# Attention scores as one-pass float32r products of exact 12-bit halves, in a transformer-like block on one Trainium2 core

## The chip, the cores and the metric

The kernel runs on one core of a Trainium2 chip. The metric is the device time of one execution in microseconds, the median over runs. TensorE (PE) multiplies matrices into eight PSUM banks, VectorE (DVE), ScalarE (ACT) and GpSimd (POOL) work on tiles, and SyncE (SP) issues the DMAs. Each engine takes its own instructions in order and waits on semaphores for the others.

## What is computed

For 16 batches of 256 positions with 256 channels, all in float32: masked attention with 16 heads of 16 channels, a normalisation with a condition's shift and gain, a time mix with two running sums over the positions, a residual, a rotation of the channels, and a gated feed-forward layer whose inputs and weights are rounded to a four-bit grid in blocks of 16. Cut to what the change touches:

```python
q, k, v = (proj(Wq), proj(Wk), proj(Wv))                  # [B, 16 heads, 256, 16]
scores = jnp.einsum('bhsd,bhtd->bhst', q, k) * scale      # scale = 16 ** -0.5
scores = jnp.where(mask[None, None, :, :], -jnp.inf, scores)
attn = jax.nn.softmax(scores, axis=-1)
out = jnp.einsum('bhst,bhtd->bhsd', attn, v)
...
out = out @ Wo.T                                           # then norm, shift and gain
...
x = x + _L0_attn_ref(_L0_cond_ref(x, ...), ...)            # time mix
x = x + _L0_ffn_ref(_L0_cond2_ref(x, ...), ...)            # rotation, feed-forward
```

The four-bit rounding makes the result sensitive to small errors ahead of it, so the products are made in full float32 throughout the kernel before.

## The kernel before

Each batch passes through nine stages, written as Python generators that yield after every few instructions. The stages are: `ask` (load x, turn it so that channels lie on partitions, project q, k and v), `attend` (scores, exponentials, products with v, division), `leave` (output projection and normalisation), `mix` (three projections, two scans, a reciprocal of 128x512), `rotate` (a projection, a rotation, rounding to the grid), `hidden` for each half of the positions (gate, up, tanh, products, rounding), `turn_h` for each half (transposes), and `down` (the last projection and the output's DMA).

What runs when is written out by hand in the text `ORDER`: 1735 steps such as `t4` (the next piece of `attend` for batch 4) or `i2` (`hidden`, second half's generator of batch 2: `h` and `i` are the two halves, `d` and `e` their transposes, `a` ask, `l` leave, `m` mix, `r` rotate, `f` down; capitals are the setup). The loop over `ORDER.split()` calls `next` on the stage named. Every engine's queue, SP's too, has its instructions in this order; several batches are on their way at the same time. Between them lie pools of buffers. PSUM has two pools of four banks: `ps_s` for scores alone, `ps_g` for all else.

In `ask`, the projection of q (L567, through `project`) goes to ScalarE twice (L626): once with the odd heads of each pair set to zero and once with the even ones (`parq`), with the factor `QSCALE`. k is copied once (L632). `attend` has a function `scores(g, kt, w)`, called four times a batch. It takes all four banks of `ps_s`. One of its four products (L656) is 32 rows, which are two heads, by 128 keys by 512 columns, which are the 256 queries of the one head and the 256 of the other. The four products stand on different rows of the array. ScalarE then takes the exponential of each bank into `w` (L665). `values` (L677) multiplies with v and a column of ones; the division follows on DVE. `qT` and `kT` have two buffers each, and `w` has two, each for both key halves of a group of eight heads.

After the last batch the kernel reads `within`, which `check` has computed from all sums of exponentials (in range or not, and whether the mask is the same for all queries). If it is 0, the whole computation runs again in the function `exact`. With the inputs given it is 1.

`load_x` (L143) and the stores of `down` (L949, L931) are issued by SP, four DMAs of 64 KB a batch each, or, for the last three batches, two of 128 KB.

Of the kernel before, what the change touches and what calls it, by code (L numbers as in the profile page):

```python
# [8 lines left out]
F32 = mybir.dt.float32  # L9
BF16 = mybir.dt.bfloat16  # L10
I32 = mybir.dt.int32
# [6 lines left out]
P = 128  # L18
# [9 lines left out]
L L L L L W1 L L a0 W5 Q Q a0 Q Q K a0 W1 W1 K K Q W1 Q L W1 a0 R a0 K a0 L W5 R L W0 W1 K K K W5 A R t0 a0 L A  # L28
W1 O t0 L a0 W3 R W5 W5 W0 M a1 A O t0 A W5 a1 R M a2 W5 t0 t0 t0 a1 R a1 t0 W0 W3 t0 R W3 W3 t0 W2 a1 t0 t0 a1
M a1 t1 a1 W0 A W3 V0 t1 t1 R R A M t0 W0 W3 a2 R t1 W0 V0 M t1 W2 t1 t0 W3 t1 t1 W4 a3 V1 W0 t0 A t0 M t0 t1 V0  # L30
t0 a3 t0 A T W2 W2 t1 T t1 V0 t1 a2 a2 a2 t1 l0 a2 t1 a2 t1 V0 l0 l0 t1 V0 a2 W4 W2 t1 l0 V0 a4 l0 l0 t2 l0 m0
t1 V1 W4 a3 t2 t2 a3 a3 m0 m0 m0 m0 m0 t2 t2 a3 W4 V1 t2 m0 m0 m0 l1 l1 l1 m0 m0 m0 l1 t2 W4 m0 m0 m0 m0 m0 t2
t2 t2 t2 l1 V0 l1 l1 a3 a3 V0 t2 t2 r0 V1 t2 W4 m1 m1 t2 W2 m1 m1 r0 a4 m1 t3 m1 W4 t3 t2 m1 m1 V1 t2 t3 t3 t2
W2 V1 r0 t3 t3 m1 m1 m1 m1 r0 V1 a4 l2 l2 m1 m1 m1 m1 t3 m1 a4 r0 t3 l2 t3 t3 a4 t3 t3 l2 r1 r1 r0 t3 r0 a4 l2
t3 t3 r1 r1 r1 l2 l2 a4 a4 a5 t3 r0 r0 a5 r0 m2 m2 t4 t4 t3 t3 m2 m2 a6 i0 i0 i0 i0 t4 i0 i0 i0 i0 i0 i0 i0 i0
i0 i0 m2 m2 m2 m2 m2 r1 r1 r1 r1 m2 t4 t4 m2 t4 r1 m2 a5 a5 a5 a5 a5 a5 m2 l3 t5 l3 t4 l3 l3 h0 m2 m2 m2 t4 t5
m2 h0 h0 h0 h0 h0 h0 l3 h0 h0 h0 r2 t5 l3 l3 V1 h0 i1 h0 r2 t4 r2 a6 V1 h0 m3 t4 i1 a7 h0 r2 i1 h1 i1 r2 t4 h1
h1 i1 t4 h1 t4 t4 h1 h1 h1 t4 m3 m3 a6 h1 h1 t5 a6 h1 r2 h1 r2 t4 t5 t4 i1 a6 r2 r2 t5 h1 h1 i1 r2 m3 a6 t5 i1
i1 i1 i1 t5 t5 h1 m3 t5 t4 t5 t5 a6 a6 m3 m3 t6 t6 m3 m3 m3 i1 i1 m3 m3 i2 i2 i2 i2 i2 m3 e0 e0 i2 i2 t6 t6 e0
i2 l4 i2 t6 i1 i2 i2 t6 h2 h2 e0 t5 m3 m3 m3 l4 h2 t6 l4 h2 m3 h2 t6 l4 h2 i2 h2 h2 h2 h2 t5 r3 h2 t5 l4 r3 a7  # L40
d0 l4 t5 h2 t6 t5 t5 l4 i2 m4 d0 d0 m4 a8 h2 t6 d0 h2 i2 a7 r3 t6 a7 a7 t6 t6 t6 t6 a7 m4 m4 m4 r3 r3 a7 a7 m4
m4 m4 t7 l5 t7 t7 l5 m4 m4 m4 m4 m4 t6 t7 l5 l5 l5 r3 m4 m4 e1 m4 m4 l5 l5 t7 t6 t6 f0 f0 f0 f0 r4 t7 r3 r4 a8
r3 e1 e1 e1 r3 f0 t7 t7 t7 d1 d1 r4 t7 t7 d1 r3 r4 i3 a9 d1 r4 i3 m5 m5 i3 i3 i3 i3 i3 a8 r4 m5 m5 i3 i3 i3 t7
a8 a8 a8 i3 i3 i3 m5 m5 t8 m5 m5 m5 l6 l6 a8 a8 l6 r4 h3 h3 l6 t8 t8 m5 h3 h3 h3 f1 m5 m5 t8 t8 i3 l6 t8 h3 f1
m5 m5 h3 h3 t7 r4 r4 r4 f1 l6 m5 m5 l6 h3 h3 h3 m5 t8 t8 t7 t7 t7 t7 t8 r5 t8 f1 t8 i4 i4 m6 t8 t8 r5 a9 d2 h3
h3 i4 d2 i4 aa i4 t8 m6 h3 t8 m6 a9 r5 r5 r5 a9 a9 a9 t8 t9 t7 d2 r5 r5 t8 t9 m6 i4 d2 r5 r5 r5 i4 i4 i4 i4 e2
m6 e2 m6 a9 i4 e2 i4 t8 e2 a9 m6 m6 l7 i4 l7 m6 m6 m6 t9 l7 l7 f2 f2 m6 m6 m6 m6 l7 l7 l7 l8 l8 t9 h4 m7 h4 l8
h4 m6 l8 m6 m7 f2 h4 f2 h4 h4 h4 h4 r6 h4 h4 l8 m7 m7 t9 t9 r6 l8 l8 h4 t9 t9 t9 r6 aa e3 f1 r6 i4 i5 h4 t9 e3
e3 e3 h4 i5 i5 i5 i5 t9 m8 r6 i5 m7 i5 i5 h4 r6 aa m7 i5 aa t9 t9 t9 ab t9 m8 i5 i5 i5 d3 f2 m7 r6 d3 h5 h5 h5
h5 h5 aa aa h5 i5 r6 r6 ta t9 h5 t9 h5 m7 h5 ta ta h5 h5 m7 h5 aa ta r6 h5 m8 aa m7 d3 d3 m7 m7 m7 m7 h5 m7 f3  # L50
m7 m7 f3 f3 f3 m8 m8 ta ta ta m8 ta m8 ta r7 r7 m8 m8 m8 ta ta d4 d4 ta i5 ta ta ta ab f3 i6 i6 i6 i6 i6 i6 i6
i6 i6 i6 i6 h6 h6 h6 h6 h6 h6 h6 h6 h6 h6 i6 ab ab ab ab d4 d4 ta tb h6 m8 h6 t9 m8 e4 e4 i6 h6 ab m8 ta ta e4
m8 ac r7 m8 l9 tb m8 i6 ab e4 f4 f4 l9 r7 h6 r7 f4 l9 l9 l9 m8 e5 tb r8 tb f4 l9 l9 f4 r8 d5 ac m9 m9 m9 r8 e5
r8 r7 r7 tb m9 la d5 r7 la la m9 m9 r8 la ac ac m9 m9 m9 m9 m9 r8 r7 tb m9 d5 m9 r7 ac m9 la d5 la la m9 ac tb
m9 tb tb i7 ma ma tb tb ad i7 i7 i7 i7 i7 i7 i7 i7 e5 e5 i7 i7 i7 tb tc tc tc m9 r8 i7 f5 f5 i7 ma f5 f5 d6 f5
r8 d6 r9 tb h7 r9 tb h7 ad r8 tb ma r8 h7 h7 h7 h7 r9 r9 h7 h7 h7 ma ma tb r9 ma r9 tc tc tc tb h7 h7 h7 ad ad
tb r9 ac ac ma ma ma ma ma h8 h8 h8 tc ma ma d6 h8 h8 d6 tc ad i8 ma ma ad r9 i8 i8 i8 i8 i8 i8 h8 h7 h8 tc i8
i8 i8 h7 ma h8 e6 h8 e6 e6 e6 h8 lb h8 h8 r9 f6 lb i8 i8 r9 f6 h8 f6 f6 ra i8 lb lb lb f6 tc tc ra e7 lb lb e7
tc h8 i8 i9 tc i9 i9 i9 ae tc ra tc mb e7 i9 mb ad ra ra td d7 e7 i9 ad tc ra i9 ae d7 td td mb mb ra tc i9 tc
i9 mb td td h9 ra i9 mb i9 mb td mb h9 mb h9 i9 h9 h9 h9 mb h9 h9 h9 d7 d7 td h9 h9 td td i9 h9 h9 lc lc td lc  # L60
af mb ae ra mb lc f7 mb mb i9 ae lc lc ra mb f7 mb lc mc ia mc h9 ia ia ia ia f7 f7 ia ia ia td ia ia ia ia mb
rb rb td td d8 td ae rb f7 ia td rb ae ae mc d8 te td mc d8 mc ae rb ia d8 rb td e8 mc td mc mc af mc e8 e8 e8
mc mc mc rb mc ld mc mc f8 te mc te te rb rb ld ld ld te ha f8 f8 ha mc ha ha rb te ha f8 ha ha ha te ha ib ha
ha ha te te te te te ib ha rc ib ib ib ib ib ib ld ld ld te rc ha ib rc ib ib e9 hb d9 rc md e9 af te rc md hb
ib hb f8 te hb md hb ib e9 md d9 af te te af e9 hb rc rc ib rc te C md af hb hb hb hb hb d9 d9 tf md af af md rc
rc hb hb le le md md tf f9 tf le md md f9 le md tf md md md md md tf tf ic ic ic ic ic f9 f9 ic ic ic le hb rd
ic le ic tf ic rd le ic me f9 rd tf ic da tf rd rd da ea hc ea hc hc rd ea ic me hc da ea tf hc rd hc tf da me
me me me tf tf hc rd me hc hc tf tf hc hc me me hc me tf tf rd tf hc me fa me me me me fa fa rd db fa me lf id
db lf fa id id id id lf lf id id id me db id id id hc lf C hd hd lf db hd lf id hd hd eb re id eb eb hd hd mf mf
id eb hd re re hd fb re hd dc hd re fb fb mf re dc fb hd mf fb mf mf re hd mf ec ec ec dc dc mf ec re fc hd mf  # L70
fc mf fc mf mf ed re fc dd fc ed mf re dd mf mf mf mf ed ie ed ie ie ie ie ie ie ie dd rf dd ie ie he C he ie he
rf rf ie C rf he ie he ie he rf fd he he he rf rf rf fd he fd he rf ee fd rf if if he he if ee if if he if if if
if hf hf if hf if if hf ee ee fd hf if hf de if hf hf hf de de de hf hf fe hf hf fe hf fe fe ef ef ef fe ef ff df
df df df ff ff ff ff ff ff
# [4 lines left out]
def kernel(  # L79
# [38 lines left out]
    QSCALE = float(D) ** -0.5  # L118

# [136 lines left out]
    odd = const.tile([P, 1], F32, tag="odd", name="odd")  # L256

# [193 lines left out]
    good = const.tile([P, (B - 1) * 2 * H], F32, tag="good", name="good")  # L451
# [3 lines left out]
    def check():  # L455
        def meet(b0, b1, dst):
            r = recs[:, b0:b1].rearrange("p b g n -> p (b g n)")
            gd = good[:, 0 : (b1 - b0) * 2 * H]
            nc.vector.tensor_scalar(gd, r, LEAST, None, ALU.is_ge)
            nc.vector.scalar_tensor_tensor(gd, r, MOST, gd, ALU.is_lt, ALU.mult)  # L460
            nc.vector.tensor_reduce(dst, gd, AX.X, ALU.min)

        meet(0, B - 1, met[:, 0:1])
        yield
        meet(B - 1, B, met[:, 1:2])
        nc.vector.scalar_tensor_tensor(met[:, 1:2], odd, 0.5, met[:, 1:2], ALU.is_le, ALU.mult)
        nc.vector.tensor_tensor(met[:, 0:1], met[:, 0:1], met[:, 1:2], ALU.min)
        yield
        pb = ps()
        nc.tensor.transpose(pb[0:1, 0:P], met[:, 0:1], ident)  # L470
        yield
        top = const.tile([1, 1], F32, tag="top", name="top")
        nc.vector.tensor_reduce(top, pb[0:1, 0:P], AX.X, ALU.min)
        nc.vector.tensor_scalar(within, top, 0.5, None, ALU.is_ge)
        yield
# [140 lines left out]

    def ask(b):
        xT = yield from enter(b)
        srcs = [xT[:, 0, :], xT[:, 1, :]]
        pq = ps()  # L620
        project(pq, wT["q"], srcs)
        yield

        qT = att_p.tile([P, E2, 2, S], F32, tag="qT", name="qT", bufs=2)
        for i in range(2):
            nc.scalar.activation(qT[:, :, i, :], halves(pq), AF.Identity, scale=parq[:, i : i + 1])  # L626
        yield
# [3 lines left out]
        kT = att_p.tile([P, E2, S], F32, tag="kT", name="kT", bufs=2)  # L631
        nc.scalar.copy(flat(kT), pk)  # L632
# [13 lines left out]
    def attend(b):  # L646
        (qT, kT), vo = qks.pop(b), v_one[b % 2]

        def scores(g, kt, w):
            quad = [bank(ps_s, "pss") for _ in range(4)]
            for r in range(4):
                rows_ = slice(32 * r, 32 * r + 32)
                nc.tensor.matmul(  # L656
                    quad[r],
                    kT[rows_, g, kt * P : (kt + 1) * P],
# [461 lines left out]
```

## Time and profile before

| | us |
|---|---|
| median of 3 runs (676.01 to 676.67) | 676.16 |
| span of the profiled execution | 674.1 |
| TensorE busy | 661.4 |
| VectorE busy | 580.2 |
| ScalarE busy | 353.8 |
| GpSimd busy | 147.8 |
| first and last products of scores (L656), start | 17.1 and 576.1 |
| time of the DMA packets, as a share of 16 engines' span | 7.6% |

The span runs from the first to the last instruction; what lies around it is the difference to the run's time, about 2 us. A busy time is the sum over an engine's instructions, overlaps counted once. In a line of a group, `x512` is the number of records, then come the busy time and the mean in ns of one record, then the idle time of that engine just before them and who ended it. PEld is the loading of weights into TensorE, which can lie beside products. In the table by stretches each row has the stretch, its length, the busy time of PE, PEld, DVE, ACT and POOL with the number of instructions, the granted clock of TensorE, the DMA share and GB/s. In a timeline a row is the start, the time and a merged run of like instructions.

### The profile page before, as it was taken

The page shows a single profiled execution, that of the slowest core. Times are in us where ns is not written, and L with a number is a line of the kernel's source. Part 1 is how long each engine was busy: PE and PEld are TensorE (multiplying, and loading weights), DVE is VectorE, ACT ScalarE, POOL GpSimd, SP SyncE. Part 2 cuts the span into 40 slices and gives each one's busy share as a digit, 9 for nine tenths or more (in the row PEclk, how much of TensorE's full clock was granted, in tenths as well). Part 3 has the DMA queues.
Part 4 walks back from the last instruction along what each step waited for, and adds up shares of the span by engine and source line. Part 5 has one row for each costly group of instructions (what it writes and reads, how often), then busy time and mean ns, then how long its engine had stood idle before and what let it go on. Part 6 is the DMA issues. An engine that isn't in the chain of part 4 may idle for free.

```text
span 674.1 us, 10439 instructions
## 1 busy us (share of the span) xinstructions
PE 661.4 (98%) x3928; PEld 467.2 (69%) x3928; DVE 580.2 (86%) x973; ACT 353.8 (52%) x777; POOL 147.8 (22%) x171
## 2 busy tenths in 40 slices
PE   6999999999999999999999999999999999999997
PEld 5567666756667766866767867675876676768776
DVE  6887988998898877888989898898998898999972
ACT  2788755564575465556345655274544654442332
POOL 4902311311222030131203120130302212131120
PEclk8999999999999999999999999999999999999999
DMA  6420000000000001000010100010000000000001
GB/s 163 129 70 1 6 12 18 1 17 0 1 18 23 11 0 33 1 15 18 1 32 1 32 1 17 1 32 1 9 8 17 1 0 17 1 17 17 16 16 37
DMA packets 37327, 13.63 MB, mean 20 GB/s; under 512 B 32900, under 2 KB 36884, under 8 KB 37268
## 3 DMA queue, kind: packets, MB, share of 16 engines
q1 hardware_dynamic: 37152, 12.85, 7.6%
q8 instruction: 33, 0.54, 0.3%
q14 instruction: 26, 0.21, 0.1%
q10 hardware_dynamic: 116, 0.02, 0.0%
HBM read 8.67 MB, written 4.19 MB: 19 GB/s over the span
## 4 chain that ended last, share of the span: by engine, by line
PE 90%; DVE 6%; DMA 1%; ACT 1%; issue 1%; SPq 0%; ACTq 0%; DVEq 0%
PE ps L567 24%; PE ps L880 21%; PE pss L656 10%; PE ps L938 9%; PE ps L677 9%; PE ps L579 8%; PE ps L543 3%; PE ps L919 2%; PE ps L843 2%; PE ps L591 1%; DMA x_sb<-in_x_dram 1%; DVE v L496 1%; DVE den L814 0%; DVE v L497 0%; PE ps L834 0%
## 5 line engine op out<-in xcount | busy, mean ns | idle before, releaser
L880 PE MATMUL ps<-guT,xqT 128*128 128x352 f32 x512 | 163.9, 463 | 0.5 <-ACT xqT L865 0.3
L665 ACT ACTIVATE w<-pss 128x512 f32<-128x512 f32 x256 | 133.8, 606 | 42.1 <-PE pss L656 41.9
L880 PEld LDWEIGHTS ps<-guT,xqT 128*128 128x128 f32 x512 | 94.1, 190 | 55.0 <-issue 3.7
L500 POOL TENSOR_TENSOR hq<-v,am 128x704 f32<-128x704 f32 (+2 forms) x40 | 55.7, 1394 | 202.8 <-DVE v L497 147.2
L656 PE MATMUL pss<-qT,kT 32*128 32x512 f32 x512 | 73.5, 640 | 0.0
L938 PE MATMUL ps<-hT,downT 128*128 128x256 f32 x312 | 70.7, 380 | 0.0
L494 ACT ACTIVATE m<-v 128x704 bf16<-128x704 f32 (+2 forms) x56 | 40.7, 729 | 53.9 <-DVE v L492 42.4
L938 PEld LDWEIGHTS ps<-hT,downT 128*128 128x128 f32 x312 | 58.9, 190 | 10.1 <-issue 0.8
L677 PE MATMUL ps<-w,v_one 128*32 128x256 f32 x1024 | 61.7, 382 | 0.0
L891 ACT ACTIVATE th<-ps 128x352 f32<-128x352 f32 x64 | 30.2, 472 | 56.2 <-PE ps L880 54.3
L814 DVE RECIPROCAL den<-den 128x512 f32<-128x512 f32 x16 | 53.6, 3348 | 0.5
L496 DVE SCALAR_TENSOR_TENSOR v<-m,v 128x704 f32<-128x704 bf16 (+2 forms) x56 | 47.0, 839 | 5.3 <-ACT m L494 5.3
L677 PEld LDWEIGHTS ps<-w,v_one 128*32 128x32 f32 x1024 | 30.1, 109 | 29.4 <-issue 6.6
L497 DVE SCALAR_TENSOR_TENSOR v<-m,v 128x704 f32<-128x704 bf16 (+2 forms) x56 | 47.1, 841 | 1.9
L546 ACT COPY hT<-ps 128x384 f32<-128x384 f32 (+1 forms) x64 | 27.1, 431 | 41.0 <-PE ps L543 40.8
L893 DVE SCALAR_TENSOR_TENSOR th<-th,ps 128x352 f32<-128x352 f32 x64 | 32.4, 506 | 13.3 <-ACT th L891 13.0
L897 DVE SCALAR_TENSOR_TENSOR h<-th,ps 128x352 f32<-128x352 f32 x64 | 33.3, 520 | 8.2 <-PE ps L880 3.9
L500 POOL TENSOR_TENSOR xq<-v,am 128x512 f32<-128x512 f32 x16 | 18.5, 1154 | 87.4 <-DVE v L497 87.4
L817 POOL TENSOR_TENSOR yT<-num,den 128x512 f32<-128x512 f32 x16 | 20.6, 1289 | 70.3 <-DVE den L814 55.5
L656 PEld LDWEIGHTS pss<-qT,kT 32*128 32x128 f32 x512 | 20.5, 182 | 22.4 <-issue 18.6
L543 PEld LDWEIGHTS ps<-ident,hq 128*128 128x128 f32 (+1 forms) x204 | 23.6, 136 | 17.3 <-issue 4.9
L687 DVE STREAM_TRANSPOSE u<-ps 128x512 f32<-128x512 f32 x32 | 22.5, 704 | 14.1 <-PE ps L677 14.1
(175 smaller groups left out, 1191.5 us busy)
## 6 DMA issues: line engine op xcount, KB each, us to landing
x_sb<-in_x_dram SPq DMA_DIRECT2D x64, 64.0 KB, 2.6
out_dram<-o_sb SPq DMA_DIRECT2D x52, 64.0 KB, 2.0
out_dram<-o_sb SPq DMA_DIRECT2D x6, 128.0 KB, 2.1
raw<-in_L_ffn_w_down_dram SPq DMA_DIRECT2D x2, 352.0 KB
raw<-in_L_ffn_w_gate_dram SPq DMA_DIRECT2D x5, 128.0 KB, 3.6
raw<-in_L_ffn_w_up_dram SPq DMA_DIRECT2D x5, 128.0 KB, 3.1
ek<-in_L_cond_Wq_dram SPq DMA_DIRECT2D x1, 256.0 KB
er<-in_L_cond_Wk_dram SPq DMA_DIRECT2D x1, 256.0 KB
```

What stands on the lines that cost most here:

```text
L496: nc.vector.scalar_tensor_tensor(v, m, 1.5 * 2.0**22, v, ALU.max, ALU.add)
L497: nc.vector.scalar_tensor_tensor(v, m, 1.5 * 2.0**22, v, ALU.max, ALU.subtract)
L500: nc.gpsimd.tensor_tensor(blk(dst), blk(v), bc(am), ALU.mult)
L543: nc.tensor.transpose(pt[0:n, (k - k0) * P : (k - k0 + 1) * P], src[:, k * P : k * P + n], ident)
L567: nc.tensor.matmul(pool_tile[:, ot * n : (ot + 1) * n], w[:, ct, ot * P : (ot + 1) * P], src[ct], start=(ct == 0), stop=(ct == E2 - 1),)
L579: nc.tensor.matmul(pool_tile[:, tt * E : (tt + 1) * E], srcT[:, ct, tt * P : (tt + 1) * P], w[:, ct, :], start=(ct == 0), stop=(ct == E2 - 1),
L656: nc.tensor.matmul(quad[r], kT[rows_, g, kt * P : (kt + 1) * P], qT[rows_, g].rearrange("p i q -> p (i q)"), start=True, stop=True,)
L665: nc.scalar.activation(w[:, kt, r].rearrange("p i q -> p (i q)"), quad[r], AF.Exp)
L677: nc.tensor.matmul(pu[32 * r : 32 * r + 32, i * S : (i + 1) * S], vo[:, kt, 8 * g + 2 * r + i, :], w[:, kt, r, i, :], start=(kt == 0), sto ...
L814: nc.vector.reciprocal(flat(den), flat(den))
L880: nc.tensor.matmul(p_[:, 0:FH], xqT[:, ct, tt * P : (tt + 1) * P], guT[:, ct, base + f * FH : base + (f + 1) * FH], start=(ct == 0), stop= ...
L938: nc.tensor.matmul(pdn[:, 0:S], downT[:, k, h * P : (h + 1) * P], hT[:, k, :], start=(k == 0), stop=(k == FK - 1))
```

## The change

Batches 0 and 1 keep their products (`whole(b)`, `NW = 2`). From batch 2 on, q (with its factor) and k are each cut into two parts. ScalarE writes the projection once as float32r, which keeps the upper 12 bits of the mantissa, and once as float32, and GpSimd subtracts the first from the second. Both parts have at most 12 bits. `spread` stores the two (512 KB) in DRAM and loads them back, in eight DMAs of 128 KB, so that each of 16 channels of a head stands on four partitions: for q the parts are high, low, high, low, for k high, high, low, low. A product over 64 rows then sums all four partial products of one head. `scores` makes eight such products of 256 columns, declared float32r, instead of four of 512 columns in float32.

`qT` and `kT` now have one buffer each (the same size in bytes as two before for `qT`), `two` one, and `w` three of half the size. The tile for `good` in `check` is taken from the pool of `mix`. One small test, made once, finds whether the low 12 bits of the float32r part are zero; `check` takes it into `within`. `ask` has twelve steps from batch 2 on instead of eight, and `ORDER` is written anew, with 1791 steps.

```diff
+F32R = mybir.dt.float32r
...
-L L L L L W1 L L a0 W5 Q Q a0 Q Q K a0 W1 W1 K K Q W1 Q L W1 a0 R a0 K a0 L W5 R L W0 W1 K K K W5 A R t0 a0 L A
...
+L L a0 Q W1 Q L L a0 L a1 a0 a0 a1 L a1 W5 Q W1 a2 K Q K a0 a2 a0 L Q W1 K a1 a1 W5 t0 t0 L a3 W1 Q a1 W5 K K V0
...
+    whole = lambda b: b < NW
...
+    tested, shared = [], {}
+
+    def parts(pt, scale):
+        two = att_p.tile([P, 2, E2 * S], F32, tag="two", name="two")
+        nc.scalar.activation(two[:, 0].bitcast(F32R), pt, AF.Identity, scale=scale)
+        nc.scalar.activation(two[:, 1], pt, AF.Identity, scale=scale)
+        yield
+        if not tested:
+            tested.append(True)
+            low = const.tile([P, 64], I32, tag="low", name="low")
+            nc.vector.tensor_scalar(low, two[:, 0, 0:64].bitcast(I32), 0xFFF, None, ALU.bitwise_and)
+            nc.vector.tensor_reduce(rest, low, AX.X, ALU.max)
+        nc.gpsimd.tensor_sub(two[:, 1], two[:, 1], two[:, 0])
+        yield
+        return two
+
+    def spread(two, tag, order):
+        kept = tc.dram_tile([2, P, E2 * S], F32, name="kept")
+        nc.sync.dma_start(out=kept.rearrange("w p n -> p w n"), in_=two)
+        dst = att_p.tile([P, 4, E2, S], F32R, tag=tag, name=tag)
+        for s in range(2):
+            for j in range(4):
+                nc.sync.dma_start(
+                    out=dst[64 * s + j : 64 * s + 64 : 4].rearrange("p u g n -> p u (g n)").bitcast(F32),
+                    in_=kept[order[j], 64 * s : 64 * s + 64].rearrange("(u d) n -> d u n", d=D),
+                )
+        return dst
...
     def ask(b):
...
+        if b == 0:
+            shared["q"] = att_p.tile([P, 4, E2, S], F32, tag="qT", name="qT")
+            shared["k"] = att_p.tile([P, 4, E2, S], F32, tag="kT", name="kT")
         pq = ps()
         project(pq, wT["q"], srcs)
         yield
-
-        qT = att_p.tile([P, E2, 2, S], F32, tag="qT", name="qT", bufs=2)
-        for i in range(2):
-            nc.scalar.activation(qT[:, :, i, :], halves(pq), AF.Identity, scale=parq[:, i : i + 1])
-        yield
+        if whole(b):
...
+        else:
+            two = yield from parts(pq, QSCALE)
+            qT = spread(two, "qT", (0, 1, 0, 1))
+            yield
         pk = ps()
         project(pk, wT["k"], srcs)
         yield
-        kT = att_p.tile([P, E2, S], F32, tag="kT", name="kT", bufs=2)
-        nc.scalar.copy(flat(kT), pk)
+        if whole(b):
...
+        else:
+            two = yield from parts(pk, 1.0)
+            kT = spread(two, "kT", (0, 0, 1, 1))
...
         def scores(g, kt, w):
             quad = [bank(ps_s, "pss") for _ in range(4)]
+            ks = slice(kt * P, (kt + 1) * P)
+            if whole(b):
...
+            else:
+                for r in range(2):
+                    for i in range(2):
+                        for s in range(2):
+                            rows_ = slice(64 * s, 64 * s + 64)
+                            nc.tensor.matmul(
+                                quad[2 * s + r][:, i * S : (i + 1) * S],
+                                kT[rows_, 2 * r + i, g, ks],
+                                qT[rows_, 2 * r + i, g, :],
+                                start=True,
+                                stop=True,
+                            )
+            yield
+            w[kt] = att_p.tile([P, 4, 2, S], F32, tag="w", name="w", bufs=3)
             for r in range(4):
...
-                nc.scalar.activation(w[:, kt, r].rearrange("p i q -> p (i q)"), quad[r], AF.Exp)
+                nc.scalar.activation(w[kt][:, r].rearrange("p i q -> p (i q)"), quad[r], AF.Exp)
                 if r % 2:
                     yield
...
-        w = [att_p.tile([P, T2, 4, 2, S], F32, tag="w", name="w", bufs=2) for g in range(E2)]
+        w = [{}, {}]
```

In the new `ORDER` the first step of `spread` for q of batch b stands behind the fourth call of `scores` of batch b-1, mostly by a few steps, and the four calls of a batch stand close together.

## The prediction

> **What bounds the kernel now.** I read the page first: shares of the engines, then the chain that ended last.
>
> ```profile
> span 674.1 us, 10439 instructions
> PE 661.4 (98%) x3928; PEld 467.2 (69%) x3928; DVE 580.2 (86%) x973; ACT 353.8 (52%) x777; POOL 147.8 (22%) x171
> PE 90%; DVE 6%; DMA 1%; ACT 1%; issue 1%; SPq 0%; ACTq 0%; DVEq 0%
> ```
>
> TensorE is busy for 98% of the span and carries 90% of the chain, so time taken off TensorE counts, unless something else then comes late. The next engine is VectorE (DVE). The table by stretches says how near it is:
>
> ```profile
> 540.00:560.00 20.00, 20.00 (x96) 15.06 (x95) 19.25 (x30) 9.76 (x23) 4.21 (x4) 1.00 0.00 0
> 600.00:620.00 20.00, 19.55 (x98) 16.55 (x99) 19.11 (x35) 6.20 (x15) 5.08 (x4) 1.00 0.06 14
> 662.00:674.10 12.10, 7.43 (x42) 6.14 (x40) 0.00 (x0) 2.77 (x9) 1.39 (x1) 0.93 0.13 40
> ```
>
> The third busy figure is DVE: 95 to 96% in late stretches, which I take as its practical ceiling; and 12.1 us follow its last instruction. Then the groups that the change touches:
>
> ```profile
> L656 PE MATMUL pss<-qT,kT 32*128 32x512 f32 x512 | 73.5, 640 | 0.0
> L665 ACT ACTIVATE w<-pss 128x512 f32<-128x512 f32 x256 | 133.8, 606 | 42.1 <-PE pss L656 41.9
> L626 ACT ACTIVATE qT<-ps,parq 128x512 f32<-128x512 f32 x32 | 20.4, 696 | 9.8 <-PE ps L567 9.7
> L632 ACT COPY kT<-ps 128x512 f32<-128x512 f32 x16 | 9.5, 593 | 9.7 <-PE ps L567 9.7
> L500 POOL TENSOR_TENSOR xq<-v,am 128x512 f32<-128x512 f32 x16 | 18.5, 1154 | 87.4 <-DVE v L497 87.4
> ```
>
> 512 records are 256 products, so a product is two records. What a call of scores really takes is seen in the timeline around one:
>
> ```profile
> 451.28 0.49 PE L543 MATMUL ps<-ident,hq 128*128 128x128 f32 x3
> 451.60 1.89 PE L579 MATMUL ps<-wt_v,xT 128*128 128x256 f32 x8
> 453.43 1.14 PE L656 MATMUL pss<-qT,kT 32*128 32x512 f32 x8
> 454.50 0.55 PE L543 MATMUL ps<-ident,hq 128*128 128x128 f32 x3
> ...
> 453.42 0.31 PEld L656 LDWEIGHTS pss<-qT,kT 32*128 32x128 f32 x8 [0.33 <-issue]
> ```
>
> Eight records of 256 columns take 1.89 us, of which the last is 0.38 (mean of its group): (1.89-0.38)/7 = 0.215 each, so their streaming ends at 451.60+1.72 = 453.32. The next work starts at 454.50. A call of scores therefore occupies TensorE for 1.18 us.
>
> **What the Trainium skill says.** "FP8 and Floating Point Precision", TensorE Precision Notes: true FP32 takes four passes, and a reduced form truncates to e10m11. The trace agrees on four: 2x0.215 for 256 columns is 0.107 per pass. No run yet shows the one-pass form. "TensorE: Matmul & The Clock Gate", LDWEIGHTS: columns/1.2 ns, whatever the rows, 107 ns for 128; three transposes (one load, one pass each) from 451.28 to 451.60 agree: 0.107 each. "TensorEngine Tiling (Array Packing)", Key Properties: tiles load and multiply in parallel, changing the mode drains; the eight loads in 0.31 us and the 0.10 us before them agree. "DMA: Bandwidth & Descriptors", Two DMAs through the same engine are not ordered: a DMA that reads what another wrote must wait for its semaphore, which the store and loads of spread must do.
>
> **Change 1, the products.** Of the 1.18 us, the four concurrent products stream 512 columns in 4 passes: 8x0.107 = 0.86; filling, draining and mode change are 0.32. The new call has eight products of 64 rows and 256 columns, in pairs on the two row halves: four steps. If pairs run together and the next load hides behind the present pass (both 0.107), they stream for 0.43, and with the same 0.32 the call takes 0.75. Gain 0.43 x 4 calls x 14 batches = 24 us. Bounds: if load and pass do not overlap, or pairs do not run together, 8x0.107 = 0.86 is back and the gain is 0; fewer than four steps of 0.107 are excluded by the column count. I take 24.
>
> **Change 2, making the halves.** ScalarE: four passes of about 0.60 us in place of two of 0.70 and one of 0.59, so +0.4 x 14 = 6 us on an engine 52% busy: hidden. GpSimd: 28 subtractions at 1.2 us (between L500's 1.154 for this shape and yT's 1.289): 34 us on an engine 22% busy. They can lengthen DVE instructions with two SBUF inputs: in this trace, scans that overlap a GpSimd instruction take 0.94 us and others 0.67. All such lengthening in the trace adds to about 19 us per 148 of GpSimd, so 34 more bring about 4 us, and the test of low bits 0.5. Beside TensorE, but see change 4. SP: nine DMAs per spread. The trace has four in 1.8 us:
>
> ```profile
> 300.64 1.80 SPq L143 DMA_DIRECT2D x_sb<-in_x_dram  x4
> x_sb<-in_x_dram SPq DMA_DIRECT2D x64, 64.0 KB, 2.6
> ```
>
> So 0.45 each, 252 of them 113 us on a queue with nothing else urgent. The packets are of 2 KB, and the trace's 128 of these took 84 ns each: 28x768x84/16 = 113 us per DMA engine, 17% more of the span, no bound. What counts is latency. From the start of the passes on ScalarE: passes 1.3, subtraction 1.3, store issue 0.45 and landing about 3.2 (16 packets of 84 ns per engine plus near 2), eight issues 3.6, last landing 2.6: 12.5 us until the scores may start. The new order, weighed by TensorE work per step (1.71 a projection, 2x1.17 a hidden pair and so on), leaves 12.7 to 19 us, in real time 4% more (from the first scores at 17.1 us to the last at 575.7, real time is 1.04 of that sum). Three batches (2, 3, 11) have 13.2 to 13.5: with queued GpSimd and SP work in front I charge 2 us in all, bounds 0 and 10. What waits behind a late load is TensorE itself, since scores stand in its order.
>
> **Change 3, fewer buffers.** With one qT and one kT the order runs a batch's four calls as a burst: 20 times only 1.71 us of TensorE work lies between two calls of batches 2 to 15, never so little before (least 2.46 after batch 1). The four PSUM banks come free after four exponentials, 4x0.603 = 2.41. They may start when half the products are in, and the last bank is wanted half a call later: 2.41-0.43+0.2 = 2.2. So TensorE waits 2.2-1.71 = 0.5 each, 0.2 of it fill and drain that it pays anyway: 20x0.3 = 6, bounds 0 and 15. Three w buffers of half size instead of two whole ones bring no later wait: the order has values before the fourth call.
>
> **Change 4, the order.** I summed DVE and TensorE work by step in both orders. After the last scores of batch 15 the old order has 85 us of TensorE and 79 of DVE left; the new one 122 and 127.5 (hidden 68, mix 32, rotate 18.5, down 7, attend 2), since attention is pulled ahead. My sum for DVE comes to 593 against 580 busy, so 127.5 is 125. At 95.5% and with the 12.1 us after it: 143. TensorE alone would need 122x1.04 plus the old tail's 10 (98.4 from 575.7 to the end, less 85x1.04): 137. So DVE sets this end and takes back 6. Between 30 and 121 us of TensorE work the new order has 97 of DVE to 92; before, 79 to 91. At 95.5% that is 100 plus a share of the lengthening, against 95 plus the waits of change 3: about 3 more. These can overlap with the waits above: 2 less.
>
> **Sum**, against its own 674.1: -24 +2 +6 +6 +3 -2 = -9, so 665. Around the span lie 676.16-674.1 = 2.1 us. The last two steps of check now come just before the end, but its few DVE instructions of 0.2 us lie beside the last output's copy and transfer (about 2 us); uncovered, 1 us. Forecast: 665.1+2.1 = 667.
>
> **Rivals.**
> - A clean gain. DVE's backlog and the bank waits are absorbed by slack in the order: 676-24+2 = 654. For it: DVE is only 86% busy overall, and TensorE ran at 100% beside a DVE at 96%. Against it: 127 us of DVE for 122 of TensorE cannot be absorbed whole.
> - Late spreads (slower). The chain store, receipt, load is longer than 12.5 us. Over the 14 batches the room is 13.2 to 20 real us; at 16.6 the waits sum to 13 and eat the gain, at 18.5 they sum to 33, so about 690. For it: SP is in order, and output stores waited up to 42.7 us for DVE there; GpSimd's subtraction stands behind products that wait for DVE. Against: single transfers land in 2 to 3.6 us.
> - The product does not stream at one pass, or pairs don't overlap: 1.18 a call remains, 667+24 = 691; were the format still taken in four passes, a call would be 4x0.43+0.32 = 2.04 and the kernel near 740, which the skill's reduced form speaks against. If the low bits are not zero after rounding, the other branch runs as well: far above 1000, outside the range.
>
> **How the numbers follow.** The forecast (658 to 674) 0.50; clean (below 658) 0.24; late spreads 0.14; no one-pass gain 0.10; other branch 0.02. 80% range 648 to 684: it cuts the other branch, most of the no-gain case and half of the late one. 0.2%, 1.4 us, is what a measurement tells here. Faster 0.75, same 0.03, slower 0.22.
>
> **What would show it.** Right: scores groups with one record per product, TensorE slot near 0.75; TensorE busy near 640; short waits of scores for exponentials; DVE at 95% over the last 130 us; loads of qT and kT landing before scores except in batches 2, 3, 11. Wrong: a slot above 1, scores waiting for DMA in most batches, or TensorE at 100% to the end (then the clean case).

## The result, and the profile after

The changed kernel takes 713.1 us (712.65 to 713.44) where the kernel before took 676.25 in the same rounds: 1.0542 times as long, 95% interval 1.0527 to 1.0557. The forecast was 667, a little faster. The products and the trip through DRAM came in near their prices, the subtractions somewhat above theirs. The order did not.

First the page of the changed kernel: span, busy times, the chain that ended last by engine, then the groups and DMAs of the change.

```profile
span 711.6 us, 10890 instructions
PE 661.8 (93%) x3928; PEld 485.2 (68%) x3928; DVE 588.6 (83%) x976; ACT 357.0 (50%) x791; POOL 174.7 (25%) x199
PE 26%; DVE 22%; issue 2%; ACT 2%; POOL 1%; DVEq 0%; POOLq 0%; ACTq 0%
L637 POOL TENSOR_TENSOR two<-two 128x512 f32<-128x512 f32 x28 | 36.9, 1316 | 84.4 <-issue 42.0
L571 PE MATMUL ps<-yT,wt_ao 128*128 128x256 f32 x128 | 38.6, 455 | 16.2 <-POOL yT L872 13.8
L710 PE MATMUL pss<-qT,kT 64*128 64x256 f32 x448 | 42.0, 304 | 0.0
kept<-two SPq DMA_DIRECT2D x28, 512.0 KB, 3.3
qT<-kept SPq DMA_DIRECT2D x112, 128.0 KB, 2.9
```

448 products are 448 records, where 256 float32 products were 512, and TensorE never sat idle before them (0.0). The chain has changed its kind. Before, TensorE had 90% of the span in it. Now it could be followed back only to 337.7 us, so that it covers about half of the span; TensorE has 26% of the span in it and VectorE 22%: the path crosses from one to the other and back. No engine is at its limit over the span. The stretches show where: from the first one-pass scores to the last ones (63 to 565 us), and from there to VectorE's last large work.

```profile
63.00:565.00 502.00, 471.40 (x2935) 344.17 (x2934) 424.08 (x680) 272.18 (x599) 120.16 (x115) 0.99 0.31 93
569.00:699.50 130.50, 121.36 (x560) 92.11 (x559) 120.33 (x201) 40.02 (x90) 23.98 (x20) 0.97 0.06 11
```

The same view of the kernel before, for its own middle (before the last scores):

```profile
57.00:576.00 519.00, 518.91 (x3105) 360.87 (x3109) 457.09 (x746) 285.32 (x625) 104.11 (x98) 1.00 0.05 11
```

Before, TensorE was busy for 518.9 of 519 us, beside a VectorE at 88%. After, TensorE is at 94% and VectorE at 84% (424 of 502): both have idle time, in the same stretch. Who waits for whom is in the view of waits. TensorE in the changed kernel (total us, times, longest):

```profile
PE ps L571 <- POOL yT L872: 13.8, 7, 2.8
PE ps L732 <- DVE res L998: 2.8, 1, 2.8
PE ps L547 <- DVE th L948: 2.8, 1, 2.8
```

VectorE in the changed kernel:

```profile
DVE u L742 <- PE ps L732: 26.2, 17, 3.6
DVE kv L849 <- PE ps L571: 10.6, 7, 3.1
DVE bs L835 <- ACT ek L842: 10.5, 5, 3.5
```

And VectorE in the kernel before, the same three waits:

```profile
DVE u L687 <- PE ps L677: 14.1, 13, 2.3
DVE kv L794 <- PE ps L567: 3.8, 6, 1.2
DVE bs L780 <- ACT ek L787: 2.2, 5, 0.7
```

VectorE waits longer: 36.8 us for TensorE's products in the first two lines, where it was 17.9, and 10.5 for ScalarE in the third, where it was 2.2. TensorE waits for what comes late from VectorE, above all for `yT`, which GpSimd makes from VectorE's reciprocal. No wait of TensorE for a DMA stands ahead of scores. One such place, in the timeline of the changed kernel:

```profile
333.03 3.35 DVE L869 RECIPROCAL den<-den 128x512 f32<-128x512 f32 x1
334.58 1.03 PE L898 MATMUL ps<-x1T,rotP 128*128 128x256 f32 x4
336.46 1.27 POOL L872 TENSOR_TENSOR yT<-num,den 128x512 f32<-128x512 f32 x1 [8.03 <-DVE den L869]
337.78 3.28 PE L571 MATMUL ps<-yT,wt_ao 128*128 128x256 f32 x8 [2.17 <-POOL yT L872]
341.10 0.69 DVE L882 TENSOR_TENSOR x1T<-xT,ps 128x512 f32<-128x512 f32 x1 [1.25 <-PE ps L571]
```

TensorE ends its rotation near 335.6 and stands for 2.17 us until `yT` comes. The eight records of L571 then take 3.28 us, where eight of this shape took 1.89 in the kernel before, and now VectorE stands for 1.25 us until they are done. The windows of the same places show why they took so long (the figure behind the busy times is TensorE's granted clock):

```profile
333.00:337.70 4.70, 2.61 (x14) 1.96 (x12) 4.64 (x4) 0.67 (x2) 1.24 (x2) 1.00 0.00 0
337.70:342.00 4.30, 4.22 (x15) 3.14 (x17) 2.91 (x6) 0.00 (x0) 0.71 (x2) 0.60 0.39 61
```

After the wait the clock was 0.60 in the mean of 4.3 us. Over the whole kernel the mean is 0.985, before 0.996.

### The profile page after: what moved, and what is told of

Same layout as the page of the kernel before. It is cut to its first block, busy times and chain, and to the rows that moved or that the text cites. A ratio compares the mean times of both kernels' runs of the same rounds, so it can differ in the third digit from the quotient of the medians.

```text
span 711.6 us, 10890 instructions
## 1 busy us (share of the span) xinstructions
PE 661.8 (93%) x3928; PEld 485.2 (68%) x3928; DVE 588.6 (83%) x976; ACT 357.0 (50%) x791; POOL 174.7 (25%) x199
## 4 chain that ended last, share of the span: by engine, by line
PE 26%; DVE 22%; issue 2%; ACT 2%; POOL 1%; DVEq 0%; POOLq 0%; ACTq 0%
PE ps L571 7%; PE ps L935 7%; DVE den L869 3%; PE ps L732 3%; PE ps L993 3%; DVE v L501 2%; DVE v L500 2%; PE ps L583 2%; DVE am L492 2%; DVE v L496 2%; PE ps L547 2%; DVE h L952 1%; PE ps L974 1%; DVE th L948 1%; DVE bs L835 1%
## 5 line engine op out<-in xcount | busy, mean ns | idle before, releaser
L935 PE MATMUL ps<-guT,xqT 128*128 128x352 f32 x512 | 169.5, 468 | 5.9 <-DVE res L998 2.1
L504 POOL TENSOR_TENSOR hq<-v,am 128x704 f32<-128x704 f32 (+2 forms) x40 | 53.9, 1348 | 204.1 <-DVE v L501 161.6
L732 PE MATMUL ps<-w,v_one 128*32 128x256 f32 x1024 | 63.5, 384 | 4.7 <-DVE res L998 2.8
L637 POOL TENSOR_TENSOR two<-two 128x512 f32<-128x512 f32 x28 | 36.9, 1316 | 84.4 <-issue 42.0
L571 PE MATMUL ps<-yT,wt_ao 128*128 128x256 f32 x128 | 38.6, 455 | 16.2 <-POOL yT L872 13.8
L500 DVE SCALAR_TENSOR_TENSOR v<-m,v 128x704 f32<-128x704 bf16 (+2 forms) x56 | 47.5, 848 | 4.3 <-ACT m L498 4.2
L501 DVE SCALAR_TENSOR_TENSOR v<-m,v 128x704 f32<-128x704 bf16 (+2 forms) x56 | 48.1, 860 | 1.9
L710 PEld LDWEIGHTS pss<-qT,kT 64*128 64x128 f32 x448 | 30.3, 185 | 22.2 <-issue 15.9
L571 PEld LDWEIGHTS ps<-yT,wt_ao 128*128 128x128 f32 x128 | 27.6, 223 | 24.7 <-POOL yT L872 16.3
L742 DVE STREAM_TRANSPOSE u<-ps 128x512 f32<-128x512 f32 x32 | 22.7, 710 | 26.2 <-PE ps L732 26.2
L948 DVE SCALAR_TENSOR_TENSOR th<-th,ps 128x352 f32<-128x352 f32 x64 | 32.1, 504 | 13.2 <-ACT th L946 12.9
L710 PE MATMUL pss<-qT,kT 64*128 64x256 f32 x448 | 42.0, 304 | 0.0
```

What stands on the lines that cost most here:

```text
L500: nc.vector.scalar_tensor_tensor(v, m, 1.5 * 2.0**22, v, ALU.max, ALU.add)
L501: nc.vector.scalar_tensor_tensor(v, m, 1.5 * 2.0**22, v, ALU.max, ALU.subtract)
L504: nc.gpsimd.tensor_tensor(blk(dst), blk(v), bc(am), ALU.mult)
L571: nc.tensor.matmul(pool_tile[:, ot * n : (ot + 1) * n], w[:, ct, ot * P : (ot + 1) * P], src[ct], start=(ct == 0), stop=(ct == E2 - 1),)
L710: nc.tensor.matmul(quad[2 * s + r][:, i * S : (i + 1) * S], kT[rows_, 2 * r + i, g, ks], qT[rows_, 2 * r + i, g, :], start=True, stop=True,)
L732: nc.tensor.matmul(pu[32 * r : 32 * r + 32, i * S : (i + 1) * S], vo[:, kt, 8 * g + 2 * r + i, :], w[kt][:, r, i, :], start=(kt == 0), sto ...
```

## The experiments

All times are medians; the ratio is to the kernel before, with its 95% interval. "The halves of batch 2" means that a kernel spreads the halves of that batch alone and uses the result for every batch from 2 on. In the new order these are q and k; in the order of before it is only q, in a tile of half the size that stands for k as well. The values are then not those of the block, and from batch 3 on the scores wait for no eviction, subtraction or transfer of their own batch.

**The order alone.** The new `ORDER` with the products of before; no halves, no trip, two more buffers (`qT` and `kT` have three each, which the new order needs when a batch's tiles are whole).

```diff
-    whole = lambda b: b < NW
+    whole = lambda b: True
...
+            qT = att_p.tile([P, E2, 2, S], F32, tag="qT", name="qT", bufs=3)
...
+            kT = att_p.tile([P, E2, S], F32, tag="kT", name="kT", bufs=3)
```

> The new order with the old products: full float32 scores for all batches, no halves, no trip through DRAM, no subtractions; the four extra steps of ask do nothing. Theory A (the new order itself sets TensorE ahead of VectorE, whatever the scores are made of): 705 to 735, with TensorE waiting for yT as in the changed kernel. Theory B (the halves and their way, that is ScalarE waiting for the store, GpSimd subtractions and loads, delay the other engines' queues, and TensorE waits for those): 675 to 690.

Measured: 723.16 us, 1.0691 (1.066 to 1.0722). The order, with the three smaller buffers of exponentials, costs 46.9 us (723.16 less 676.25), with not one product changed. That is more than the whole change lost. The last scores start at 574.3 in it and the span ends at 721.9. TensorE waits 8.2 us for `yT`.

```profile
L704 PE MATMUL pss<-qT,kT 32*128 32x512 f32 x512 | 82.0, 640 | 0.0
```

A part of it belongs to the old products. These 512 records took 73.5 us in the order of before (L656), and here their weight loads wait 9.1 us for exponentials in 28 places, where the kernel before shows no such wait: the four calls of a batch stand close together and the banks come free late. In the changed kernel it is 4.5 us in 11 places. From these figures I estimate that 5 to 9 of the 46.9 us are not paid by the changed kernel; the step from this run to the new products looks larger by as much.

**No trip through DRAM.** The changed kernel, with the halves of batch 2; all halves are still made.

```diff
     def spread(two, tag, order):
+        if tag in shared:
+            return shared[tag]
...
+        shared[tag] = dst
         return dst
```

> The changed kernel with the store and loads made only once, for batch 2; batches 3 to 15 read batch 2's spread halves (their scores are those of batch 2), while ScalarE and GpSimd still make the halves of every batch. Theory A: no gain, 703 to 714. Theory B with the trip as its core: 670 to 695. If only the subtractions matter: 703 to 714 as well, told apart by the third run.

Measured: 710.82 us, 1.0509 (1.0478 to 1.0539). The trip costs 2.3 us by the medians, near the 2 that the prediction charged, though the intervals of the two kernels still overlap. TensorE's idle time (span less busy time) is 49.2 us, for 49.8 with all trips; before the change it is 12.7.

**The products in the order of before.** The old `ORDER` (the extra yields of `ask` taken out), the new products with the halves of batch 2, all halves made. The changed kernel itself can't stand in the old order: by the text of the program, with single `qT` and `kT` the engines would wait for each other in a circle. This was not run.

> The old order with the new products from batch 2 on: halves made for every batch by ScalarE and GpSimd, but only batch 2's q is stored and spread, and all later scores are made of it, so that no transfer can be late. Theory A: the gain of the products comes out, 650 to 664. Theory B with the subtractions and the ScalarE passes as its core: 676 to 700.

Measured: 673.11 us, 0.9943 (0.9915 to 0.9971). So the old order takes the new products without the 47 us, but their gain shrinks to 3. That was less than expected, and the next four runs take it apart.

```diff
-        nc.gpsimd.tensor_sub(two[:, 1], two[:, 1], two[:, 0])
+        if b == NW:
+            nc.gpsimd.tensor_sub(two[:, 1], two[:, 1], two[:, 0])
```

> The order of before with the products of 64 rows and the two ScalarE passes for the halves, but without GpSimd's subtractions (only batch 2 has them; so the low halves are left out, and as in the run before the scores of all batches use the spread halves of batch 2). Theory C, the 28 subtractions on GpSimd lengthen VectorE's operations by 12 us and VectorE's lateness eats the gain of the products: VectorE's busy time falls from 592 to about 580 us and the time to 655 to 664 us. Theory D, the gain is lost elsewhere (banks of scores, buffers of exponentials, records that overlap less): 669 to 674 us, as with the subtractions (673).

Measured: 664.02 us, 0.9819 (0.9803 to 0.9836): 9.1 us faster than with the subtractions. VectorE's lines by form, with the subtractions and then without:

```profile
L500 DVE SCALAR_TENSOR_TENSOR v<-m,v 128x704 f32<-128x704 bf16 x34 | 36.0, 1058 | 1.2
L635 POOL TENSOR_TENSOR two<-two 128x512 f32<-128x512 f32 x28 | 40.8, 1456 | 124.8 <-ACT two L629 124.8
```

```profile
L500 DVE SCALAR_TENSOR_TENSOR v<-m,v 128x704 f32<-128x704 bf16 x34 | 33.1, 973 | 1.2
```

The same 34 instructions took 1058 ns each and then 973. In sum VectorE's busy time fell from 592.4 to 579.6.

Products alone: the evictions of before and the new products with the halves of batch 2; no other halves are made.

```diff
+            if b == NW:
+                spread(parts(pq, QSCALE), "s", (0, 1, 0, 1))
+            else:
+                old = att_p.tile([P, E2, 2, S], F32, tag="qT", name="qT", bufs=2)
+                for i in range(2):
+                    nc.scalar.activation(old[:, :, i, :], halves(pq), AF.Identity, scale=parq[:, i : i + 1])
+            qT = shared["s"]
```

> The order of before and the evictions of before, but the scores of batches 2 to 15 as products of 64 rows on the spread halves of batch 2 (the halves of the other batches are left out). It has the products' gain and nothing of its price except the third buffer of exponentials. Prediction's term: 24 us less than 676, so 650 to 656 us. If TensorE is not what bounds the order of before alone, because VectorE (580 us busy of 674) is late behind it: 660 to 670 us, with more gaps on TensorE than the 26 us of before.

Measured: 665.03 us, 0.9832 (0.9816 to 0.9849), in the higher of the two ranges expected: the products' gain does not come out whole. TensorE's idle time is 18.9 us, for 12.7 in the kernel before. ScalarE's passes for the halves are in the run before this one and not in this one, and cost little: the two times differ by 1.0 us, and the waits for the one trip, 3.7 us here and 0.9 there, could hide some 2 us more. A call of scores in its timeline:

```profile
452.64 0.59 PE L570 MATMUL ps<-xm,wt_ak 128*128 128x256 f32 x2
453.16 0.74 PE L713 MATMUL pss<-s 64*128 64x256 f32 x8
453.83 0.86 PE L938 MATMUL ps<-guT,xqT 128*128 128x352 f32 x2
```

From the start of a call to the start of the next work it is 0.67 us, also as the median of its calls; in the kernel before the median is 1.07. That is 0.40 a call and 22 us for 56 calls.

The subtractions alone, in the kernel before:

```diff
+        if b >= 2:
+            half = qT[:, 0].rearrange("p i (c n) -> p (i c) n", n=P)
+            nc.gpsimd.tensor_sub(half, half, nil.unsqueeze(1).to_broadcast([P, 4, P]))
```

> The kernel before with 28 subtractions of a zero tile on GpSimd (128x512, two a batch from batch 2 on, on the evicted q and k in place; the result is unchanged). Theory C: VectorE's busy time grows by 8 to 14 us and the time by 6 to 14 us, to 682 to 690. If GpSimd's work does not matter: 676 to 678 us.

Measured: 684.68 us, 1.0122 (1.0105 to 1.0139); VectorE's busy time 597.1 (580.2 before). Scores wait a little for these subtractions too, since they are made in place, so the 8.3 us over the kernel before in the same rounds (676.36) are an upper figure for what they cost by way of VectorE.

And the buffers of exponentials alone, in the kernel before:

```diff
-        w = [att_p.tile([P, T2, 4, 2, S], F32, tag="w", name="w", bufs=2) for g in range(E2)]
+        w = [{}, {}]
...
+            w[kt] = att_p.tile([P, 4, 2, S], F32, tag="w", name="w", bufs=3)
```

> The kernel before with the change's buffers of exponentials alone: three of 8 KB a partition in the place of two of 16 KB. The prediction's third part priced the fewer buffers at 6 us (0 to 15) in the new order. In the order of before: 676 to 682 us; the scores' waits for exponentials or banks grow by what the time grows by.

Measured: 679.03 us, 1.0037 (1.0024 to 1.0049): 2.5 us. From there to the products alone it is 14.0 us.

**The new order without the subtractions.** Edit as in the old order, on the kernel without the trip.

> The new order with one trip through DRAM (batch 2 only) and without GpSimd's subtractions (the low halves are left out, except in batch 2). Theory C says that in the new order VectorE is later still, so each microsecond taken from it counts: 694 to 702 us against 710.8 with the subtractions. If the new order is slow for another reason than VectorE's lateness (the order of TensorE's own work, banks): 707 to 711 us.

Measured: 706.28 us, 1.0453 (1.0434 to 1.0471). Only 4.5 us of the 710.8 go, between the two ranges expected, and the runs scatter (702.87 to 708.15). The lighter VectorE (575.3 for 588.2) helps, but this is a small part of the loss.

**Work taken off VectorE.** The reciprocal of the mixing's denominator is left out in the changed kernel and in the kernel before, and, later, in the run of the order alone.

```diff
-        nc.vector.reciprocal(flat(den), flat(den))
```

> The changed kernel without VectorE's reciprocal of the mixing's denominator (L869, 16 x 3.35 = 54 us of VectorE; the division of the mixing is left out, y is a product). Theory V: VectorE's lateness is what the new order pays, so the time falls by 25 to 40 us, to 673 to 688, and TensorE's gaps to under 40 us. If VectorE's lateness is not the cause (banks, or the order of TensorE's work): 702 to 713.

> The kernel before without the same reciprocal (the division of the mixing is left out). TensorE is busy 98% there, so theory V expects little: 666 to 675 us. A fall as large as in the new order would say that both orders wait for VectorE alike.

Measured: the changed kernel 669.88 us, 0.9905 (0.9889 to 0.9922), which is 43.2 less than with the reciprocal, a little more than expected. The kernel before 675.13, 0.9983 (0.9976 to 0.999), 1.1 less. The order of before has almost nothing to gain from a lighter VectorE; the new one gains 0.78 us for each of 55.5 us. The same stretches, in the changed kernel without the reciprocal:

```profile
63.00:532.70 469.70, 461.81 (x2932) 340.69 (x2934) 379.04 (x667) 271.85 (x599) 119.85 (x115) 1.00 0.32 99
532.70:656.00 123.30, 122.34 (x585) 93.69 (x582) 114.10 (x203) 44.22 (x103) 26.10 (x22) 1.00 0.07 14
```

TensorE is at 98% up to the last scores, which start at 532.7 and not at 565; the wait for `yT` is no longer in the view of waits, and the clock is 1.00. The values behind the missing division are far off in these runs. That the time depends on values was not tested by itself; the runs without a rounding, below, which leave the division in, point the same way.

The run of the order alone without the reciprocal:

> The new order with the products of before and no halves, as in the run of the order alone (723), without the reciprocal of the mixing's denominator (the division is left out). Theory V: the order's price is VectorE's lateness, so most of the 47 us goes: 680 to 692 us, and the distance to the changed kernel without the reciprocal (669.9) is then the products' gain, 12 to 20 us. If the order costs TensorE time of another kind: above 700.

Measured: 689.45 us, 1.0202 (1.0185 to 1.0219), 33.7 less than with it. With VectorE eased, the changed kernel lies 19.6 us under the order alone: this is the products' gain, net of halves and trip. But 14.3 us over the kernel before without the reciprocal (675.13) are left. In this run the weight loads of scores wait 10.2 us for exponentials in 31 places, so a part of the order's price is these waits for banks and not VectorE; the rest was not taken apart.

The reciprocal stands in the chain that leads to `yT`. To see whether the place matters, about as much was taken from VectorE elsewhere: the two rounding passes of the hidden layer's quantization (`none_put` is the default of `put`, which only the hidden layer's tiles replace).

```diff
+        if not (tag == "hq" and put is not none_put):
-        nc.vector.scalar_tensor_tensor(v, m, 1.5 * 2.0**22, v, ALU.max, ALU.add)
-        nc.vector.scalar_tensor_tensor(v, m, 1.5 * 2.0**22, v, ALU.max, ALU.subtract)
+            nc.vector.scalar_tensor_tensor(v, m, 1.5 * 2.0**22, v, ALU.max, ALU.add)
+            nc.vector.scalar_tensor_tensor(v, m, 1.5 * 2.0**22, v, ALU.max, ALU.subtract)
```

> The changed kernel without the two rounding passes of the hidden layer's quantization (L500 and L501 for the 32 tiles of 128x704, 32 x 1.86 = 60 us of VectorE; that rounding is left out). It takes about as much from VectorE as the reciprocal (54 us), but away from the mixing's own chain. Theory V1, VectorE's whole load counts in the new order: 30 to 45 us faster than 713, so 668 to 683. Theory V2, only the length of the chain from the mixing to yT counts: less than 15 us, so 698 to 713.

> The kernel before without the same two rounding passes (the rounding of the hidden layer's quantization is left out): as without the reciprocal, TensorE bounds it, 672 to 676 us. A fall of over 10 us would say that the order of before has waits for VectorE too.

Measured: in the new order 691.27 us, 1.0217 (1.0196 to 1.0238), 21.8 less; in the order of before 676.19, 1.0002 (0.9993 to 1.001), nothing. It fell between the two theories. In the new order VectorE's load counts in both places (0.38 us for each of 57.4 us taken here), and in the chain to `yT` it counted twice as much. TensorE's wait for `yT` is still there in the changed kernel without the rounding:

```profile
PE ps L574 <- POOL yT L875: 10.0, 5, 2.7
```

**Two attempts to mend the order.** In the first, TensorE comes to L571 later. For instance, in batch 8 (the moved steps are those of `r8`):

```diff
-m8 h5 r8 m9 h5 la tb tb r6 tb tb i5 ab h5 r8 h5 i5 i5 tb
+m8 h5 m9 h5 la tb tb r6 tb tb i5 ab h5 h5 i5 i5 r8 r8 tb
```

> The changed kernel whole, but TensorE comes to the output projection of the mixing (L571 with yT) later: the first step of rotate is moved back by 1.5 to 8 us of TensorE's own work in 15 of 16 batches (as far as the four banks allow), with VectorE's addition behind it where it must. Theory Y, the new order meets yT too soon and nothing else is wrong there: the gaps ahead of that projection fall from 18 to under 8 us and the time from 713 to 698 to 705. Theory V, VectorE is late as a whole, so that a wait avoided here comes back at the next product that needs VectorE: 709 to 713, with the gaps ahead of other products larger.

Measured: 736.83 us, 1.0887 (1.0857 to 1.0917), slower by 24 us, which neither theory had foreseen. The moves were of up to 8 us of TensorE's work. The wait for `yT` did shrink, to 2.2 us, but the projection now comes late for VectorE, whose addition behind it (L879 here, L882 in the changed kernel) waits 24.6 us where it waited 5.3. TensorE's idle time rose from 49.8 to 68.3 us.

```profile
DVE x1T L879 <- PE ps L568: 24.6, 12, 4.6
DVE u L739 <- PE ps L729: 22.9, 15, 3.6
```

In the second, VectorE takes the values out of their banks (`u`) later. About half of the 32 transposes moved, by 0.5 to 7 us of VectorE's work, and nine calls of scores came up to 1.7 us later on TensorE with them.

```diff
-t9 h4 t8 m7 r6 e3 r6 m7 aa t9 t9 t9 t9 t9 t9 aa t9 r5 t9
+t9 h4 m7 r6 e3 r6 m7 aa t9 t9 t9 t9 t9 aa t9 r5 t8 t9 t9
```

> The changed kernel whole, with VectorE's transposes of the weighted values out of their banks (L742) moved later in VectorE's order, 25 of 32, past 0.5 to 7 us of VectorE's other work each (73 us in sum), as far as divide allows. In the changed kernel VectorE waits 26 us for these values. Theory V with the reading that the two engines wait for each other in turn at places like this: those waits fall under 12 us, VectorE comes earlier to the mixing, and the time falls from 713 to 695 to 706. If what TensorE waits for is not behind these waits: 711 to 716; and if the moved transposes hold up what follows (divide, the output projection): above 716.

Measured: 725.84 us, 1.0719 (1.0687 to 1.0751), slower by 12.7. VectorE's wait for the values fell from 26.2 to 18.3 us, its wait at `kv` rose from 10.6 to 18.6. In both runs the wait that was aimed at became shorter and another became longer.

**The reciprocal on GpSimd**, as a power of -1, to ease VectorE in a whole kernel.

```diff
-        nc.vector.reciprocal(flat(den), flat(den))
+        nc.gpsimd.tensor_tensor(flat(den), flat(den), mone.to_broadcast([P, E2 * S]), ALU.pow)
```

> The changed kernel whole, with the reciprocal of the mixing's denominator (L869) made on GpSimd as a power of -1 (128x512) in the place of VectorE. Without the reciprocal the changed kernel took 669.9. If GpSimd's power of 128x512 takes no more than about 5 us, the chain to yT grows little and VectorE keeps its 54 us: 670 to 690 us, near or under the kernel before (676). If it takes 8 us or more, the chain from the mixing to yT grows by more than the lighter VectorE gives, and what else GpSimd does (halves, norms, quantization) waits behind it: above 713.

Measured: 1957.97 us, 2.8947 (2.8899 to 2.8995). One power of 128x512 takes 82 us:

```profile
L871 POOL TENSOR_TENSOR den<-den,mone 128x512 f32<-128x512 f32 x16 | 1311.2, 81948 | 59.0 <-DVE den L869 53.6 <-PE ps L573 5.3
```

It tells nothing of the order, and with it the question of place against load stays half open: that the place counts is shown by two runs of different work, not by the same work in two places.

## Why the prediction was wrong, point by point

The parts from the kernel before to the changed one, each the difference of two runs: the order 46.9, then products, evictions and one trip -16.9 (723.2 to 706.3), subtractions 4.5 (to 710.8), the other trips 2.3 (to 713.1). With runs that scatter by up to 5 us (those at 706.3) the small parts are rough. The run of the order has the fewer buffers of exponentials too, so the prediction's term for it is 13 (6 for buffers, 6 and 3 for the order, 2 taken off for overlap, with a share of GpSimd's effect on VectorE in it). For the others it has -24, nothing of its own for the subtractions, and 2.

- **Change 1, the products: right.** One record per product; a call takes the time of four steps, so pairs run together and the load is hidden. The prediction put a call at 1.18 before and 0.75 after, counted from the end of the streaming ahead; from start to start it is 1.07 and 0.67. The gain per call is 0.40 for 0.43, 22 us for 24. In the kernel's time it gave 14.0 in the order of before, where the products of batch 2 also waited 3.7 us for their one trip, and 16.9 in the new order, where the old products had their own waits for banks (5 to 9 us by the estimate above). The rival without a one-pass gain fell. The other branch did not run either (713 us, not far above 1000), so the low 12 bits that the kernel tests were zero.
- **Change 2, the halves: the chain right, one term too small.** ScalarE's passes cost little, as said. The trip costs 2.3 us for 2, and the slower rival, late spreads, did not happen: the loads landed 2.9 to 3.0 us after issue, near the estimate of 2.6, and scores didn't wait for them. (That rival's 690 is also too low by its own sum: 33 us of waits in place of 2 make 698.) The subtractions lengthened VectorE's work by 12.8 us in the order of before and 12.9 in the new one (busy times with and without), for 4 predicted. The price of an average microsecond of GpSimd, taken from all of GpSimd's work in the trace, was too low for these subtractions by a factor of three; why was not tested.
- **Change 3, fewer buffers: within its bounds.** The buffers of exponentials cost 2.5 us in the order of before. For the bursts of calls that come with the single `qT` and `kT`, the weight loads of scores in the changed kernel wait 4.5 us for exponentials in 11 places; this is idle time of the loads, beside which products run, and no more than a bound. 6 was the forecast.
- **Change 4, the order: this step failed.** The prediction added DVE's and TensorE's work over two long stretches and charged the difference: 6 us at the end, 3 early on, 2 less for overlap, 7 in all. Even without what belongs to buffers and banks (2.5 us and the 5 to 9 of the estimate), the order alone cost about five times as much. Its picture of the end was right. From the last scores on it had 143 us; measured, from 564.9 to 711.6, it is 146.7, with VectorE at 92% up to 699.5 (the table of stretches). What was wrong lies ahead of it. With 143 us behind them and a span of 665, the last scores had to start at 522; they started 43 us later. The prediction's sums leave no idle time on TensorE in that stretch beyond the few microseconds charged; in the order of before there was almost none. In the new order both engines idle there, VectorE 16% and TensorE 6% of the time, and what TensorE did was stretched by a lower clock (0.99 in the mean of the stretch). The wait that the views name is short, 1 to 3 us, and lies at single hand-overs from one engine to the next. Sums over 100 us can't show it: they say what an order needs at least, not what it takes.

Why is VectorE late? Less work on VectorE gives 43 us (reciprocal) and 22 us (rounding) in the new order and 1 and 0 in the old one. So it is shown by two pairs of runs that the new order pays for VectorE's work where the old one does not. The order alone falls by 34 us as well, so it isn't the halves. That the waits alternate, each engine for the other, is a reading of the timeline above and of the first moved order, where TensorE's wait for `yT` shrank and VectorE's for the product behind it grew; in the second, one wait of VectorE was traded for another. Why VectorE comes late at just these places is not shown. Which steps of the 1791 would have to stand elsewhere was not found.

Of the other signs named, TensorE's busy time was to fall to 640 and is 661.8. With the reciprocal left out it is 648.7: these 13 us are not work. About 10 of them are the stretches at half clock described below, by an estimate; the rest is open. The clean rival (654) rested on slack that this order does not have; a lighter VectorE brought it only to 670.

No kernel that does the whole computation came out ahead of the kernel before. The best of the others (664.0) leaves out the low halves and all trips but one, in the order of before. Whether the whole spread tiles can stand beside its double buffers was not tried.

## What to carry to other kernels

When a change comes with a new order, run the new order with the old work first: here this one run shows a loss larger than the whole. A kernel in which one engine is at 98% can have an order balanced to the microsecond, so price a reordering by the hand-overs between in-order engines, not by sums of work. And ask of each engine what a microsecond taken from it would bring: next to nothing for the 50 us and more taken from VectorE before, 0.4 to 0.8 of each in the new order.

## What was not expected of the hardware

- **A short wait of TensorE costs twice.** In the changed kernel TensorE stood still for 1.85 to 2.84 us in eight places after the start-up. Six of them were followed by 3.4 us at a granted clock of 0.50, as behind the wait at 337.8 above (from 338.3 to 341.7). That makes an estimate of six times 1.7, about 10 us. The kernel before and the changed one without the reciprocal have no such stretch between their first 14 and their last 3 us. The Trainium skill, "TensorE: Matmul & The Clock Gate", What's actually happening, has the clock halved after an idle window of about 3.4 us and restored after as long a busy one. The half and the 3.4 us of low clock agree; but here waits of about 2 us, shorter than that window, were enough in six places of eight.
- **GpSimd slows VectorE by more than its share.** 28 subtractions of 37 to 41 us in all lengthened VectorE's busy time by 13 us. The Trainium skill, "GPSIMD Engine Reference", Specifications, says that their SBUF interfaces are shared, with contention for VectorE's instructions with two SBUF inputs. The trace agrees (973 to 1058 ns for one such form), and VectorE's reductions of 128x704, which have one input, stayed at 884 ns in both runs.
- **A power on GpSimd took 82 us** for 128x512, where its products of the same shape take 1.3.
